# Layer 0 of two attention layers: the bias product of two rows in seven block products instead of eight

## The chip, the cores and the metric

The kernel runs on one core of a Trainium2 chip. The metric is the device time of one execution in microseconds (us), from outside the program; the profile's span runs from the first to the last instruction of one profiled execution. All arithmetic is float32.

## The reference

Two residual layers act on a tensor x of 128 rows of 256 tokens of 256 channels. The change is in the first, here cut to what matters (`_gn` is a group normalization over all rows and tokens):

```python
bias = jnp.einsum('nijz,zh->nhij', pair_repr, bias_proj)[:, None]
gate = jax.nn.sigmoid(msa_repr @ gate_proj).reshape(bs, s, r, head, c)   # 8 heads of 32
q, k, v = jnp.split(msa_repr @ qkv_proj, 3, axis=-1)
sim = jnp.einsum('nsqhc,nskhc->nshqk', q, k) * scale
sim = jax.nn.softmax(sim, axis=-1)
sim = sim + bias                       # added after the softmax, the same for all rows s
attend = jnp.einsum('nshqk,nskhc->nsqhc', sim, v) * gate
out = attend.reshape(bs, s, r, cm) @ out_proj
# x = x + layer0(_gn(x)); then x = x + layer1(_gn(x)), a banded attention of 4 heads
```

Since the bias is added after the softmax, `attend` is a softmax part, exp(sim) @ v divided by the sums, and a bias part, bias @ v. The bias is the same for every row, so for two rows together the bias part is, for each head, a 256 x 256 matrix (query by key) times the values of both rows: a product of 2 x 2 blocks by 2 x 2 blocks (key halves, query halves, the two rows).

## The kernel before

A first stage (to about 205 us) reads pair_repr and x, builds the bias in SBUF (`bias_sb`: partition = key within a half, then key half, head, query) and the statistics of x. Then a loop over the 128 rows s computes layer 0, and a second loop layer 1. In layer 0 the orders of TensorE (PE), ScalarE (ACT), VectorE (DVE) and of the DMA queue of SyncE (SP) are those of the program text (`tc.manual_schedule`); GpSimd (POOL) gets its order from the scheduler. A TensorE tile of 128 x 32 is a column strip: four products for four heads, or four quarters of an output, run side by side in the four strips, and float32 takes two instructions for each product.

Every row has the same frame, and rows go in pairs i = s // 2, of an even and an odd row. In row s, in TensorE's order:

- `scores(s, 0)`: scores of four heads (`sim`), which ScalarE turns into `ex` by exp; VectorE joins the two key halves (`both`, L862).
- `sum_heads(s - 1)` (`zs`, L885), the sums over keys; `divide(s - 1)` takes the reciprocal on VectorE (`rz`, L904), sends it to DRAM and back, spread over partitions (`near`, L910).
- `attend(s - 1)` (`av`, L872), the softmax part; then `scores(s, 1)`, the other four heads.
- a `stretch`, which computes two of the four projections for the next pair in seven products each (`two_of_them`): q and k in even rows, v and g (the gate) in odd rows. Each product adds into one of two halves of a PSUM bank, and ScalarE copies a half out (`take`: "15" after products 1 and 5, "6" and "7" into `mid`, "34") before the next product adds into it. GpSimd then adds the copies together (L631, L634). In odd rows the output projection of an earlier pair (`po`, seven products too, taken by VectorE at L704 to L726) is woven in.
- `bias_products(s - 1)` (`bv`, L872), the bias part of one row in two halves, put between the last products of the stretch by `between`.

On VectorE, `gated(s - 2)` heads the row: the bias part is added (L964, reading `bv` in PSUM), and the gate is applied (L965, writing `at`). `normal(s + 4)` transposes and normalizes a coming row (L553, L821). `weighted(s - 1)` multiplies `av` by `near` (L953). ScalarE's `totals` (L930) reads the sums `zs` once with an accumulator read. GpSimd's `row_sums` (L582 to L584) forms four sums of blocks that the seven products need: `ts` for the projections, `att` for the output.

PSUM has five banks in a ring for scores and projections and one each for `av`, `zs` and `bv`.

Of the kernel before, what the change touches and what calls it, by code (L numbers as in the profile page):

```python
# [15 lines left out]
P = 128  # L16
# [23 lines left out]
def conv_preact_kernel(  # L40
# [594 lines left out]

    def two_of_them(pool, f, g, name, po, rest, between):

        for p in (f, g):
            p.open()
            p.product(1)  # L640
            p.product(5)
            p.take("15")
        rest()
        twos = proj_bank(f"p2{name}")
        two = pool.tile([P, 2, R], F32, tag="two", name=f"two{name}", bufs=1)
        f.product(2, twos[:, 0, :], first=True)
        next(po, None)
        for p in (f, g):
            p.product(3)
            p.product(6)  # L650
            p.take("6")
            next(po, None)
        f.product(7)
        f.take("7")
        g.product(2, twos[:, 1, :])
        next(po, None)
        g.product(7)
        g.take("7")
        f.product(4)
        f.take("34")  # L660
        next(po, None)
        for work in between[:1]:
            work()
        g.product(4)
        g.take("34")
        nc.scalar.copy(two, twos)
        next(po, None)
        for work in between[1:]:
            work()
        next(po, None)  # L670
        for n, p in enumerate((f, g)):
            p.add_two(two[:, n, :])
            p.add_mid()
# [103 lines left out]
    with ExitStack() as both:  # L777
# [4 lines left out]
        quarters1["o"] = Quarters(st1, w_out_t, 0, "1o")  # L782
        big1 = both.enter_context(tc.tile_pool(name="big1", bufs=2))
        ygs, pools = {}, {}
        rz_far = dram.tile([2, 2, 4, R], F32, name="rz_far")
        rz0_far = dram.tile([2, A, 2, R], F32, name="rz0_far")

# [11 lines left out]
        with ExitStack() as lay0:  # L799
# [5 lines left out]

            xns, tss, res, ats, ats_t = {}, {}, {}, {}, {}

# [24 lines left out]
            def scores(s, half):  # L832
# [3 lines left out]
                for kt in range(2):  # L836
                    for c in range(2):
                        for j in range(4):
# [6 lines left out]
                            )  # L845
                ex = att.tile([P, 4, 2, R], F32, tag="ex", name=f"ex{s}_{half}", bufs=4)
                both = att.tile([P, 4, R], F32, tag="both", name=f"both{s}_{half}")
# [15 lines left out]

            def products(to, s, weights, halves=range(2)):

                i, r = divmod(s, 2)
                v = res["v", i]
                for half in halves:
                    for kt in range(2):
                        for j in range(4):  # L870
                            c0 = kt * P + j * D0
                            nc.tensor.matmul(  # L872
                                to[D0 * j : D0 * (j + 1), half, :],
                                lhsT=v[:, 2 * r + half, c0 : c0 + D0], rhs=weights(4 * half + j, kt),
                                start=(kt == 0), stop=(kt == 1),
                            )
# [13 lines left out]

            def bias_products(s):

                if s < 0:
                    return ()
                bv0 = hd[s] = ps_av.tile([P, 2, R], F32, tag="bv", name=f"bv{s}")
                return tuple(
                    lambda half=half: products(bv0, s, lambda h, kt: bias_sb[:, kt, h, :], (half,)) for half in range(2)
                )

            def divide(s, zs):  # L900
# [3 lines left out]
                nc.vector.reciprocal(rz, zs[:, 0, :])  # L904
                near = att.tile([P, 2, R], F32, tag="near", name=f"near{s}")
                if s < S - 1:
# [48 lines left out]
            def gated(s):  # L955
# [4 lines left out]
                if r == 0:  # L960
                    ats[i] = row.tile([P, 4, R], F32, tag="at", name=f"at{i}")
                st[s]["at"] = at = ats[i][:, 2 * r : 2 * r + 2, :]
# [11 lines left out]
            def output(i, amid):  # L974

                g, k = divmod(2 * i, XG)
                if k == 0:
                    outs[g] = big1.tile([P, XG, 2, R], F32, tag="o", name=f"o{g}")
                return Output(
# [5 lines left out]
            def finish(s):  # L985

                g, k = divmod(s, XG)
                if k == 0:
                    outs[g] = big1.tile([P, XG, 2, R], F32, tag="o", name=f"o{g}")
                nc.vector.tensor_tensor(outs[g][:, k], st[s]["po"], st[s]["xt"], ALU.add)  # L990
                settle(s, k, k, S // 2 - 1 + k % 2)
# [12 lines left out]

            def stretch(names, i, po=iter(()), rest=lambda: None, between=()):

# [3 lines left out]
                for w, p in zip(names, (f, g)):  # L1010
                    res[w, i] = p.to
                two_of_them(row, f, g, f"{names}{i}", po, rest, between)

# [6 lines left out]
            with tc.manual_schedule(  # L1020
# [4 lines left out]
                sum_rows(0)  # L1025
                stretch("qk", 0)
                for s in range(2, 4):
                    normal(s)
                stretch("vg", 0)
                sum_rows(1)  # L1030
                most1 = Most(st1, stats1, 3, 1)
                for s in range(S):
# [6 lines left out]
                    if s % 2 == 1:  # L1039
                        e = res["g", s // 2]  # L1040
                        nc.scalar.activation(e, e, AF.Tanh, scale=0.5)
                    attend(s - 1)
                    join_tiles(s, 0, 2)
                    if s % 2 == 0:
                        settle_pair((s - 4) // 2)
# [4 lines left out]
                    if s == 4:  # L1050
                        for weights in quarters1.values():
                            weights.sum()
                    late = (lambda: join_tiles(s, 1, 0), lambda: join_tiles(s, 1, 2), lambda: weighted(s - 1), lambda: least(s - 1))
                    bias = bias_products(s - 1)

# [6 lines left out]
                    if s % 2 == 1 and s > 1:  # L1062
                        out_sums((s - 3) // 2)
                        po, late = output((s - 3) // 2, late), ()
                    if s < S - 2:
                        stretch(("qk", "vg")[s % 2], s // 2 + 1, po, rest, bias)
                    else:
                        rest()
                        for work in bias:
                            work()  # L1070
                        for _ in po:
                            pass
                    for work in late:
                        work()
                    if s % 2 == 1 and s < S - 1:
                        sum_rows((s + 3) // 2)
                load1(0)
                load1(1)
# [10 lines left out]
                attend(S - 1)  # L1089
                for work in bias_products(S - 1):  # L1090
                    work()
                spread_last(S - 1)
# [16 lines left out]
        with ExitStack() as lay:  # L1109
            ps_av = psum(lay, "1", 4, 0)  # L1110
            pools["yg"] = lay.enter_context(tc.tile_pool(name="yg1", bufs=1))
            row = lay.enter_context(tc.tile_pool(name="row1", bufs=4))
# [368 lines left out]
    with tc.If(sure < P):  # L1481
        with ExitStack() as lay:
# [4 lines left out]
            for t in range(2):  # L1487
# [4 lines left out]
                out=bv_row.rearrange("p a b -> p (a b)"), in_=b_in[2 * C : 3 * C].partition_broadcast(P)  # L1492
            )
            stats2 = one.tile([P, 2, S // 2, 6], F32, name="stats2")

# [166 lines left out]
```

## Time and profile before

| | |
|---|---|
| median of 3 runs | 3122.66 us (3121.35 to 3122.96) |
| profiled execution | 3117.48 us, its span 3115.8 us |
| TensorE clock granted | 0.993 of full speed |
| pairs of layer 0 | from 205.9 us; layer 1's first work at 2044.1 us |
| group of instructions of the bias product (L872 bv) | 4096 instructions, 267.7 us busy |
| group of the attend product (L872 av) | 4096 instructions, 244.5 us busy |

Times are from the start of the span. "Busy" of a group is the time in which at least one of its instructions ran. The matrix instructions of the four strips overlap, so the mean of one (379 ns for 256 columns, 273 ns for 128 columns) is not what it adds to the queue; for that, the distance from one step's start to the next is read. PEld is TensorE's loading of weights, which runs beside the products. A "pair" below is the stretch of time from the first scores of an even row to those of the next even row.

### The profile page before, as it was taken

To read this page: it belongs to the slowest core of one execution; us is meant where nothing else is said; L and a number is where in the kernel's file an instruction comes from. 1 tells how busy PE (TensorE), PEld (TensorE's weight loads), DVE (VectorE), ACT (ScalarE), POOL (GpSimd) and SP (SyncE) were. 2 spreads that over 40 slices of the span, in tenths; PEclk is the share of its full clock that TensorE was granted. 3 is DMA by queue.
4 is the path that set the end of the run, shared out by engine and by line. 5 is a ranking of instruction groups with operands and counts; after the bars stand their busy time and mean duration, and the time that the engine had idled before them with its cause. 6 is when DMAs were issued, how large, how long until landed. Compare 5 with 4: busy or idle time off the path is not lost.

```text
span 3115.8 us, 135366 instructions
## 1 busy us (share of the span) xinstructions
PE 3038.3 (98%) x59661; PEld 1995.8 (64%) x59661; DVE 2176.2 (70%) x4327; ACT 1828.6 (59%) x4065; POOL 1718.3 (55%) x1660
## 2 busy tenths in 40 slices
PE   7889999999999999999999999999999999999997
PEld 4556566556656665665666566567777777777775
DVE  4667777777777777777777777746666666666665
ACT  4666666666666666666666666545555555555553
POOL 3035555545454555545454555457776777777774
PEclk9999999999999999999999999999999999999999
DMA  9942222222222222222222212124444444444443
GB/s 373 424 130 58 61 48 63 62 62 49 64 61 50 61 64 61 47 64 61 56 56 64 61 49 63 50 63 95 100 103 98 104 95 100 104 99 103 96 99 71
DMA packets 383716, 279.87 MB, mean 90 GB/s; under 512 B 285216, under 2 KB 352272, under 8 KB 376976
## 3 DMA queue, kind: packets, MB, share of 16 engines
q1 hardware_dynamic: 382224, 268.76, 33.1%
q8 instruction: 470, 7.70, 1.1%
q0 software_dynamic: 752, 2.36, 0.2%
q14 instruction: 126, 1.03, 0.1%
q10 hardware_dynamic: 144, 0.00, 0.0%
HBM read 202.38 MB, written 68.66 MB: 87 GB/s over the span
## 4 chain that ended last, share of the span: by engine, by line
PE 92%; DMA 4%; DVE 2%; ACT 1%; issue 0%; POOL 0%; SPq 0%; DVEq 0%; ACTq 0%; POOLq 0%
PE sim L840 9%; PE av L872 7%; PE bv L872 7%; PE p1v L1184 7%; PE p1q L590 7%; PE po L590 6%; PE p1k L590 6%; PE p1o L590 6%; PE pq L590 6%; PE pv L590 6%; PE pk L590 5%; PE pg L590 5%; PE zs L885 4%; DMA pr<-in_L_conv_pair_repr_dram 4%; PE 1sim L1205 3%; PE 1av L1246 3%
## 5 line engine op out<-in xcount | busy, mean ns | idle before, releaser
L853 ACT ACTIVATE ex<-sim 128x512 f32<-128x512 f32 x1024 | 550.2, 608 | 318.4 <-PE sim L840 318.4
L862 DVE TENSOR_TENSOR both<-ex 128x512 f32<-128x512 f32 x512 | 402.0, 813 | 15.1 <-ACT ex L853 15.0
L634 POOL TENSOR_TENSOR q<-q,midq 128x512 f32<-128x512 f32 x64 | 82.0, 1281 | 443.3 <-ACT q L628 443.3
L634 POOL TENSOR_TENSOR v<-v,midv 128x512 f32<-128x512 f32 x64 | 81.6, 1276 | 415.6 <-ACT v L628 415.6
L840 PE MATMUL sim<-q,k 32*64 32x256 f32 x8192 | 288.9, 387 | 1.4 <-ACT ex L853 1.3
L872 PE MATMUL bv<-bias_sb,v 128*32 128x256 f32 x4096 | 267.7, 379 | 0.0
L904 DVE RECIPROCAL rz<-zs 128x256 f32<-128x256 f32 x128 | 224.3, 1753 | 32.9 <-PE zs L885 32.9
L872 PE MATMUL av<-ex,v 128*32 128x256 f32 x4096 | 244.5, 379 | 0.1
L1215 POOL TENSOR_TENSOR 1p<-1ex,seen 128x768 f32<-128x768 f32 x127 | 231.5, 1823 | 12.8 <-ACT 1ex L1213 12.8
L1184 PE MATMUL p1v<-w_in_t,1xn 128*64 128x128 f32 x4096 | 236.2, 273 | 0.1
L1184 PEld LDWEIGHTS p1v<-w_in_t,1xn 128*64 128x64 f32 x4096 | 231.4, 137 | 6.1 <-issue 0.5
L840 PEld LDWEIGHTS sim<-q,k 32*64 32x64 f32 x8192 | 151.9, 131 | 127.4 <-issue 104.1
L697 ACT ACTIVATE 1q<-p1q,bqk 128x256 f32<-128x256 f32 x192 | 90.9, 473 | 240.8 <-PE p1q L590 129.7
L582 POOL TENSOR_TENSOR 1ts<-1xn 128x512 f32<-128x512 f32 x64 | 81.4, 1271 | 231.6 <-ACT 1xn L1145 231.6
L872 PEld LDWEIGHTS av<-ex,v 128*32 128x32 f32 x4096 | 133.4, 110 | 87.9 <-issue 0.6
L872 PEld LDWEIGHTS bv<-bias_sb,v 128*32 128x32 f32 x4096 | 133.6, 110 | 87.5 <-DVE both L862 0.4
L964 DVE TENSOR_TENSOR t<-bv,t 128x512 f32<-128x512 f32 x128 | 87.9, 687 | 131.0 <-PE bv L872 130.9
L1315 DVE TENSOR_TENSOR 1at<-1av,1near 128x512 f32<-128x512 f32 x128 | 82.6, 686 | 136.3 <-DMA 1near<-rz_far 115.3
L1222 POOL TENSOR_TENSOR 1zp<-1p 128x512 f32<-128x512 f32 x127 | 162.4, 1279 | 10.0
L726 DVE TENSOR_TENSOR o<-po,xt 128x256 f32<-128x256 f32 x189 | 80.3, 425 | 98.9 <-PE po L590 98.9
L1191 ACT COPY 1v<-p1v 128x512 f32<-128x512 f32 x128 | 75.0, 586 | 125.1 <-PE p1v L1184 125.1
L346 DVE BATCH_NORM_STATS2 stats<-xs 128x6 f32<-128x128 f32 x512 | 100.3, 278 | 65.3 <-DMA xs<-in_x_dram 65.3
(320 smaller groups left out, 7826.1 us busy)
## 6 DMA issues: line engine op xcount, KB each, us to landing
pr<-in_L_conv_pair_repr_dram SPq DMA_DIRECT2D x32, 1024.0 KB
xs<-in_x_dram SPq DMA_DIRECT2D x16, 2048.0 KB
x<-o SPq DMA_DIRECT2D x64, 512.0 KB
yg<-x SPq DMA_DIRECT2D x64, 512.0 KB
out_dram<-1o SPq DMA_DIRECT2D x256, 128.0 KB
near<-rz_far SPq DMA_DIRECT2D x508, 64.0 KB
xg<-in_x_dram SPq DMA_DIRECT2D x252, 128.0 KB
1near<-rz_far SPq DMA_DIRECT2D x124, 256.0 KB
```

Of the source, the lines that this page charges most:

```text
L346: nc.vector.bn_stats(out=stats[:, g, n, :], in_=xs[:, 0:k, g * CG : (g + 1) * CG])
L590: nc.tensor.matmul(out[cols], lhsT=lhsT[:, cols], rhs=rhs, **flags)
L634: nc.gpsimd.tensor_tensor(self.to[:, 2:4], self.to[:, 2:4], self.mid, ALU.add)
L840: nc.tensor.matmul(sims[j][KB * c : KB * (c + 1), kt, :], lhsT=k[p0 : p0 + D0, 2 * r + half, k0 : k0 + KB], rhs=q[p0 : p0 + D0, 2 * r + ha ...
L853: nc.scalar.activation(ex[:, j], sims[j], AF.Exp, scale=1.0 / math.sqrt(D0))
L862: nc.vector.tensor_tensor(both[:, j : j + 2], ex[:, j : j + 2, 0, :], ex[:, j : j + 2, 1, :], ALU.add)
L872: nc.tensor.matmul(to[D0 * j : D0 * (j + 1), half, :], lhsT=v[:, 2 * r + half, c0 : c0 + D0], rhs=weights(4 * half + j, kt), start=(kt == ...
L885: nc.tensor.matmul(zs[strip(j), 0, :], lhsT=place0[:, half, :], rhs=both[:, j, :], start=(half == 0), stop=(half == 1),)
L904: nc.vector.reciprocal(rz, zs[:, 0, :])
L1184: nc.tensor.matmul(ps[KB * half : KB * (half + 1), b, :], lhsT=xns[i][:, 2 * r + kt, KB * b : KB * (b + 1)], rhs=w_in_t[:, kt, 2 * C + P * ...
L1215: engine.tensor_tensor(p.rearrange("p j (r c) -> p (j r) c", c=WROW)[:, :, 0 : 2 * WSTEP] .rearrange("p r (t c) -> p r t c", c=WSTEP)[:, : ...
L1222: engine.tensor_tensor(zp, p[:, :, 0:R], p[:, :, R : 2 * R], ALU.add)
```

## The change

The bias part is now computed for two rows at once, by `biased(i)`, in seven block products instead of eight (a product of 2 x 2 blocks in the manner of Strassen and Winograd). Its parts:

- The sums of bias blocks are kept: `sum_bias` forms three new blocks and overwrites one block of `bias_sb` with a difference, once, by VectorE in row 0. The block that is overwritten is stored to DRAM first (`bias_far`), and read back in the branch for unusual data at the program's end.
- The sums of the values are formed for each pair by GpSimd (`sum_values`, four operations of 128 x 256), after the odd row's stretch.
- Each of the seven products is eight matrix products of 128x32 weights by 128 columns. Two products at a time use the two halves of the PSUM bank `bv`; after each product, ScalarE copies (2, 6, 5 and 4) or VectorE adds (1, 7 and 3), into SBUF tiles `bv0`, `bv1` and `midb`. `gated` reads the bias part from there instead of from PSUM.
- The products are spread over the pair: 2, 1 and 6 in the even row's stretch; 5 in the odd row between `sum_heads` and `attend`; 7, 3 and 4 in the odd row's stretch. They belong to the pair itself, not to the row before.
- The order of a stretch is now written as a string. In it fA and gA are products 1 and 5 with their copy, x is ScalarE's last exp and `totals`, f and g with a number are products (2 of g with the copy of both), b a bias product, p an output product, d one of the late VectorE works (two joins, `weighted`, `least`). In even rows product 2 of f moves from behind gA to behind f7; in odd rows product 2 of g moves from behind f7 to behind g4.
- Buffers: `ex` 3 instead of 4, `near` 1 instead of 2, `at` 1 instead of 2, the layer 0 output tile `o` 1 instead of 2 (its pool `big1` is opened for layer 1 only). New tiles: `vt`, `bv0`, `bv1`, `midb`, `bias_sums`.
- In the last two rows, which have no stretch, the bias products stand among the output products; nothing of the bias part is left behind the loop.

```diff
+    PLAIN = "fA gA x f2 p f3 f6 p g3 g6 p f7 b p g7 f4 p b g4 p g2 b p"
+    EARLY = "fA gA x d b f3 f6 g3 g6 d f7 f2 g7 f4 b d g4 g2 d b"
...
-                ex = att.tile([P, 4, 2, R], F32, tag="ex", name=f"ex{s}_{half}", bufs=4)
+                ex = att.tile([P, 4, 2, R], F32, tag="ex", name=f"ex{s}_{half}", bufs=3)
...
+            bias_of = {
+                1: bias_blocks[0, 0], 2: bias_blocks[1, 0], 4: bias_blocks[1, 1],
+                3: bias_sums[:, 2], 5: bias_sums[:, 0], 6: bias_sums[:, 1], 7: bias_blocks[0, 1],
+            }
+            def sum_bias():
+                w00, w10, w01, w11 = (bias_blocks[kb, m] for m in range(2) for kb in range(2))
+                s1, s2, s4 = (bias_sums[:, n] for n in range(3))
+                nc.vector.tensor_tensor(s1, w01, w11, ALU.add)
+                nc.vector.tensor_tensor(s2, s1, w00, ALU.subtract)
+                nc.vector.tensor_tensor(s4, w10, s2, ALU.subtract)
+                nc.vector.tensor_tensor(w01, w00, w01, ALU.subtract)
+            def sum_values(i):
+                v = res["v", i]
+                vts[i] = row.tile([P, 4, 2, P], F32, tag="vt", name=f"vt{i}", bufs=1)
+                by_key = v.rearrange("p (r h) (k c) -> p k r h c", r=2, k=2)
+                t = vts[i]
+                for h in range(2):
+                    nc.gpsimd.tensor_tensor(
+                        t[:, 0::2, h], by_key[:, :, 1, h], v[:, h::2, 0:P], ALU.subtract
+                    )
+                nc.gpsimd.tensor_tensor(t[:, 1], by_key[:, 1, 1], t[:, 0], ALU.subtract)
+                nc.gpsimd.tensor_tensor(t[:, 3], by_key[:, 1, 0], t[:, 1], ALU.subtract)
+            def biased(i):
...
+                for n in (2, 1, 6, 5, 7, 3, 4):
+                    acc = 1 if n in (2, 3, 5) else 0
+                    for half in range(2):
+                        for j in range(4):
+                            nc.tensor.matmul(
+                                ps[strip(j), acc, half, :],
+                                lhsT=stationary[n][:, half, strip(j)], rhs=bias_of[n][:, 4 * half + j, :],
+                                start=(n <= 2 and half == 0), stop=(n in (2, 3, 4)), skip_group_check=True,
+                            )
...
+                    if n == 2:
+                        nc.scalar.copy(to[0][:, 0], ps[:, 1])
+                    elif n == 1:
+                        nc.vector.tensor_tensor(to[0][:, 0], ps[:, 0], to[0][:, 0], ALU.add)
+                    elif n == 6:
+                        nc.scalar.copy(mid, ps[:, 0])
+                    elif n == 5:
+                        nc.scalar.copy(to[1][:, 1], ps[:, 1])
+                    elif n == 7:
+                        nc.vector.tensor_tensor(to[1][:, 1], ps[:, 0], to[1][:, 1], ALU.add)
+                    elif n == 3:
+                        nc.vector.tensor_tensor(to[1][:, 0], ps[:, 1], mid, ALU.add)
+                    else:
+                        nc.scalar.copy(to[0][:, 1], ps[:, 0])
+                    yield
...
-                near = att.tile([P, 2, R], F32, tag="near", name=f"near{s}")
+                near = att.tile([P, 2, R], F32, tag="near", name=f"near{s}", bufs=1)
...
+                    if s % 2 == 0:
+                        bias = biased(s // 2)
+                    else:
+                        next(bias)
                     attend(s - 1)
                     join_tiles(s, 0, 2)
+                    if s == 0:
+                        sum_bias()
...
-                    bias = bias_products(s - 1)
...
-                    if s % 2 == 1 and s < S - 1:
+                    if s % 2 == 1 and s < S - 2:
                         sum_rows((s + 3) // 2)
+                        sum_values(s // 2 + 1)
...
-                for work in bias_products(S - 1):
-                    work()
```

## The prediction

> **What bounds the kernel now.** I read the busy times first, then the stretches, then the chain that ended last, then the timeline of one pair of rows. The page gives TensorE 98% of the span and nobody else over 70%. The stretch answer (columns: length; busy time of TensorE, weight loads, VectorE, ScalarE, GpSimd; clock, DMA share, GB/s) shows the steady part of layer 0.
>
> ```profile
> PE 3038.3 (98%) x59661; PEld 1995.8 (64%) x59661; DVE 2176.2 (70%) x4327; ACT 1828.6 (59%) x4065; POOL 1718.3 (55%) x1660
> ...
> 231.18:2004.85 1773.67, 1773.61 (x38692) 1067.29 (x38689) 1324.88 (x2163) 1120.53 (x2419) 917.04 (x869) 1.00 0.25 58
> ```
>
> 62 pairs in 1773.67 us are 28.61 us a pair, and TensorE lacks 0.06 us in all. So a pair costs what TensorE's queue costs, and a change counts only as it shortens that queue or makes it wait. The chain over one pair is TensorE alone, with each step's own length:
>
> ```profile
> 1009.27 0.86 PE pk L590 x16
> 1010.13 0.43 PE p2qk L590 x8
> 1010.56 0.94 PE pq L590 x16
> ...
> 1014.09 0.86 PE bv L872 x16
> ```
>
> A product of a 128x256 operand is 0.43 us; a half of a row's bias product (16 instructions) is 0.86. The 0.94 hides a wait. The timeline (start, length, engine, work; in brackets the idle time before and what ended it) shows it, and the places where the others are tight:
>
> ```profile
> 1004.64 1.20 DVE L965 SCALAR_TENSOR_TENSOR at<-g,t 128x512 f32<-128x512 f32 x1
> ...
> 1007.42 1.53 DVE L862 TENSOR_TENSOR both<-ex 128x512 f32<-128x512 f32 x2
> ...
> 1010.43 0.16 PEld L590 LDWEIGHTS pq<-xn,sums_q 128*32 128x32 f32 x8 [0.35 <-ACT q L622]
> ...
> 1011.20 0.45 ACT L930 ACTIVATE z<-zs 128x256 f32<-128x256 f32 x1
> 1011.37 1.28 DVE L862 TENSOR_TENSOR both<-ex 128x512 f32<-128x512 f32 x2
> 1011.47 0.26 ACT L930 ACTIVATION_READ_ACCUMULATOR z<-zs 128x1 f32 x1
> ...
> 1011.63 0.37 ACT L624 COPY midq<-pq 128x256 f32<-128x256 f32 x1
> ...
> 1012.05 0.27 PEld L590 LDWEIGHTS pq<-ts,sums_q 128*32 128x32 f32 x8 [0.16 <-ACT midq L624]
> ...
> 1014.82 1.28 POOL L634 TENSOR_TENSOR q<-q,midq 128x512 f32<-128x512 f32 x1 [7.02 <-ACT q L628]
> ...
> 1023.64 0.62 PE L590 MATMUL pv<-sums_v,xn 128*32 128x128 f32 x16
> 1023.89 0.42 DVE L726 TENSOR_TENSOR o<-po,xt 128x256 f32<-128x256 f32 x1 [0.43 <-PE po L590]
> 1024.07 0.62 PE L590 MATMUL pv<-sums_v,ts 128*32 128x128 f32 x16
> ```
>
> See: ScalarE runs without a gap up to midq, and a weight load of the q product 7 starts 0.05 after midq ends. GpSimd is idle for 7 us before q+midq. VectorE is 0.43 early at an odd row's first output add. A v product, 16 instructions 128 columns wide, starts 0.43 after the one before.
>
> **What the skill says.** The Trainium skill, "TensorEngine Tiling (Array Packing)", Key Properties: changing the tiling mode drains TensorE. The new products keep the 128*32 form, so no change of form is added; the trace has the price at the scores (bias half at 1015.21, scores at 1016.18: 0.97 for 0.86). The skill, "SBUF — State Buffer", SBUF: two separate sides: VectorE and GpSimd share a port pair; an operation with two SBUF inputs, or in a 2-port mode, and a GpSimd operation exclude each other ("the other fully blocks"). The trace agrees: two joins of `both` take 1.53 where they meet the end of GpSimd's work and 1.28 where they don't, and the gating (L965) 1.20 beside GpSimd; the bias add (L964, from PSUM) takes 0.68 beside busy GpSimd.
>
> **The change part by part.** Times are those of the pair above (even row from 1003.37, odd from 1016.18).
>
> *Bias product on TensorE.* Before, four halves a pair, 4 x 0.86 = 3.44. After, 7 products of 16 instructions 128 columns wide. Their price is the v product's 0.43, the same weights and width; different moving data in the four strips is what the old bias product has too, at full rate. 7 x 0.43 = 3.01: -0.43 a pair, over 64 pairs **-27.5 us**. If the rate failed by 0.05 a product, 0.35 a pair would be gone.
>
> *ScalarE: four copies of 128x256 a pair*, 1.5 us where it is idle 10.5 of 28.6 (stretch of one pair: busy 18.07). Product 5's sits after the tanh, 6's and 4's at the end of a stretch, before scores it waits 0.7 to 1.7 us for: nothing, and if that idle time went, up to 0.27 each. Product 2's is different: it goes between the read of the totals and midq. One 256-wide operation pushes the next by 0.27 (1011.20 to 1011.47). So midq ends at 1012.27, not 1012.00, while product 7 of q, in the same place since bias product 2 replaces product 2 of q before it, has its turn at 1012.18. From the 0.94 above: the q copy ended (9.77+0.61) just when that step was due, and the queue lost 0.08. So q's product 7 starts at 1012.35: **+0.17 a pair**, x63 = +10.7. Bounds 0.05 to 0.3.
>
> *VectorE: three adds of 128x256 from PSUM a pair* (0.42, the output adds' row), with 7.2 us idle of 28.6. Two come in odd rows between output adds: 0, as each meets 0.3 to 1.3 us of waiting for `po`; if that cover went, 0.42 would be late for the next output product. The third (product 1) gates product 6, which adds into the same half bank. With product 7's wait, product 1 ends at 1014.8, the add at 1015.25, product 6's turn is 1015.43: 0.1 spare, if the add starts at once. Ahead of it in VectorE's queue stand the joins of the second scores; behind it the scaling by the sums, already waiting for its DMA (it began at 1013.64) and not needed until 1016.3.
>
> *GpSimd: four sums of 128x256*, 0.73 each (ts, L583, without contention): 2.9 us, in the 7 us idle before 1014.82; bounds 2.9 to 4.8 (1.19 each, L631 beside VectorE). Their readers: product 6 at 1015.4, sums ready by about 1012.6. One goes ahead of adding product 2 to v; that still ends near 1008.7, before bias product 2 at 1009.95. The cost is the port. Also the bias add now reads SBUF twice, so it takes part. For the even row I count a gating that ends 0.9 later (two operations, each held about half a GpSimd operation), the first two joins +0.55, the normalization +0.3: the second joins end at 1014.4 instead of 1012.65. That is 0.4 before product 1's add: 0. For the odd row the gating ends 0.6 later, the reciprocal, which waits for the sums (1018.37), about as before; then out_sums start later and meet both joins in full, +0.65, so the first output add, 0.43 early, is about 0.2 late: VectorE still finishes 0.1 before the next output product needs it. 0, bounds -0 to +0.3 a pair.
>
> *Buffers.* ex 4 to 3: the third buffer is free when the attend product is through, and the scores stand behind that on TensorE. near, at: their readers precede the next write on the same engines by whole rows. o: its store (issued 1011.90) shares in traffic that is over by 1018 (stretch 1018 to 1020: 6 GB/s), the next write is at 1024. All 0; without that cover the output add would wait for the store.
>
> *SP:* one more store of 512 KB, once, ahead of x loads that are four rows early: 0. The reload stands in a branch that isn't taken.
>
> *Start.* VectorE sums the bias, 4 operations of 128x1024, 1.2 each (twice 0.68 less one start), and sharing the port with seven GpSimd operations: 8 us or so in row 0, ahead of the normalization, the joins and product 1's add. Product 6 then stands about 4 us, and the ts sums delay two products by 0.9: **+5** (2 to 8).
>
> *End.* Row 126 has three products in a row without cover: product 6 waits for an add behind bn_aggr (1011.05+1.82 after 2000), +2.6, of which the following wait for the joins returns half; the last row's bias leaves the path to `near` (-0.65); layer 1's first tiles now wait for the last store: +1.5 against the plain count (-1 to 4).
>
> **Sum:** -27.5 + 10.7 + 5 + 1.5 = **-10.3 us**. The profiled execution took 3117.48 (span 3115.8), 5.2 below the median 3122.66; the same difference from the median gives 3112.4.
>
> **Rivals.** *Full gain:* ScalarE's copy starts are 0.05 to 0.1 closer and product 7 doesn't wait: -27.5+6.5 = -21, 3102. For: 0.1 of slack stood before midq; against: the queue has no gap there. *GpSimd's sums run into q+midq (slower):* if the even row's chain is 1.3 us later than I count, the last join (start 1013.7) asks for the port after q+midq took it at 1015.0. It ends at 1016.85, product 1's add at 1017.2, and product 6 waits 1.85 us for it in each pair: 62 x 1.85 = +115, less 10: 3225. It decides from a GpSimd sum of about 1.1 instead of 0.73. For: L631's 1.19; against: 1.3 us of room. *Small waits add up (no change or a little slower):* 0.1 to 0.3 a pair at product 6 and the first output add, where spare is 0.1: +6 to +19, so 3118 to 3131.
>
> **How the numbers follow.** Forecast 0.47, full gain 0.13, small waits 0.27, collision 0.13. 0.2% is 6.2 us, about what a measurement of this kernel can tell from no change. Faster takes the forecast, the full gain and none of the rest: 0.60; small waits split 0.12 same, 0.15 slower; with the collision slower is 0.28. The range 3098 to 3131 leaves out the collision and a few per cent below.
>
> **What would show it.** The steady pair at 28.35 (28.17 without product 7's wait); 0.17 more before q's product 7, put down to midq; no TensorE wait on the add of product 1; joins at L859 longer, about 0.9 mean. Wrong, if TensorE idles on VectorE at bias product 6 or at `po`, or bias products start over 0.45 apart.

## The result, and the profile after

The changed kernel took 3123.47 us (median; 3121.14 to 3128.69), the kernel before 3121.93 on the same chip (3116.97 to 3124.77): ratio 1.0009, 95% interval 1.0000 to 1.0017. The forecast of 10 us less did not come. The profiled execution took 3121.14, its span is 3119.4 us.

The stretches of the changed kernel's profile (columns as in the prediction): the first two pairs, the 61 pairs that follow, the last two rows with what leads into layer 1, and layer 1.

```profile
207.10:241.13 34.03, 26.98 (x572) 16.38 (x569) 20.26 (x23) 20.39 (x43) 19.62 (x16) 0.90 0.04 10
241.13:270.93 29.80, 29.27 (x677) 18.10 (x673) 26.29 (x39) 19.69 (x45) 21.33 (x20) 1.00 0.16 39
270.93:2008.79 1737.86, 1737.60 (x40997) 1103.38 (x40993) 1535.30 (x2314) 1174.58 (x2624) 1183.03 (x1099) 1.00 0.25 59
2008.79:2050.09 41.30, 33.38 (x542) 19.60 (x539) 33.07 (x60) 14.03 (x31) 8.54 (x10) 0.96 0.25 79
```

| stretch | before | after | difference | forecast |
|---|---|---|---|---|
| ahead of the first scores | 205.92 | 207.10 | +1.2 | 0 |
| first two pairs | 53.86 | 63.83 | +10.0 | +6.0 |
| 61 pairs | 1745.07 | 1737.86 | -7.2 | -15.9 |
| last two rows and what leads into layer 1 | 39.24 | 41.30 | +2.1 | -0.5 |
| layer 1 | 1071.7 | 1069.3 | -2.4 | 0 |
| span | 3115.8 | 3119.4 | +3.6 | -10.3 |

The forecast column splits the prediction's sum by stretch, which the prediction itself did not do: 5 for the sums of the bias, and 1.3 for bias products that now stand in the first pair and no longer at the end; -0.26 for each steady pair; what is left of the sum falls to the last rows. Layer 1's work did not change; over all profiles below it takes 1069.1 to 1072.5. Ahead of the first scores stand only a store, the first pair's sums of the values and a new order of the same products. The first scores begin at 205.0 and 205.9 in the two profiles with the old row loop, at 206.1 to 207.5 in the six that have the new loop alone, and at 208.1 to 209.0 in the three that also sum the bias there (e4, f1, f2). So the change, and the early sums too, may cost a microsecond or two ahead of the loop; no run parts that from the spread.

The 61 pairs gain, but half of what was forecast: the steady pair is **28.47** us (28.60 before, 28.35 forecast). TensorE's busy time fills the stretch in both kernels, so that column can't show where the rest went. The chain over one even row of the changed kernel can (start, length of the step in the queue, step):

```profile
1018.28 0.44 PE pbv L933 x16
1018.72 0.99 PE pq L590 x16
1019.71 0.86 PE pk L590 x16
1020.58 0.60 PE pq L590 x8
...
1023.77 0.49 PE pbv L933 x16
```

A bias product is 0.44 where nothing is in its way, a q product 0.43. Three steps are longer than that count: the two q products 3 and 6 (0.99; 0.94 before), q's product 7 (0.60; 0.43 before) and bias product 6 (0.49). The timeline of that row shows what each is near:

```profile
1016.45 2.07 DVE L859 TENSOR_TENSOR both<-ex 128x512 f32<-128x512 f32 x2
...
1018.64 0.16 PEld L590 LDWEIGHTS pq<-xn,sums_q 128*32 128x32 f32 x8 [0.19 <-ACT q L622]
...
1019.77 0.43 ACT L943 COPY bv<-pbv 128x256 f32<-128x256 f32 x1
...
1020.12 0.37 ACT L624 COPY midq<-pq 128x256 f32<-128x256 f32 x1
...
1020.54 0.16 PEld L590 LDWEIGHTS pq<-ts,sums_q 128*32 128x32 f32 x8 [0.44 <-ACT midq L624]
...
1023.05 0.42 DVE L945 TENSOR_TENSOR bv<-pbv,bv 128x256 f32<-128x256 f32 x1 [0.63 <-PE pbv L933]
...
1023.59 0.41 PEld L933 LDWEIGHTS pbv<-bias_sums,vt 128*32 128x32 f32 x16 [0.30 <-issue]
```

Product 2's copy (L943) stands ahead of midq, and q's product 7 waits for midq, as forecast. But the q product 3 is late too, which was not, and product 6's first weight load begins 0.12 after product 1's add has ended, with "issue" as the reason: no other engine's work ended there.

The start, in the timeline of row 0:

```profile
212.23 1.75 DVE L901 TENSOR_TENSOR bias_sums<-bias_sb 128x1024 f32<-128x1024 f32 x1
...
217.25 1.75 DVE L904 TENSOR_TENSOR bias_sb<-bias_sb 128x1024 f32<-128x1024 f32 x1
...
221.26 3.41 DVE L859 TENSOR_TENSOR both<-ex 128x512 f32<-128x512 f32 x2
222.42 1.70 POOL L634 TENSOR_TENSOR k<-k,midk 128x512 f32<-128x512 f32 x1
...
224.60 0.41 DVE L945 TENSOR_TENSOR bv<-pbv,bv 128x256 f32<-128x256 f32 x1
225.16 1.08 PE L933 MATMUL pbv<-bias_sums,vt 128*32 128x128 f32 x16 [5.25 <-DVE bv L945]
226.17 2.01 PE L837 MATMUL sim<-q,k 32*64 32x256 f32 x32
```

The four sums take 6.8 us of VectorE. The two joins come behind them and meet GpSimd's adding of q and k: 3.41 for what takes 1.28 alone. TensorE waits 5.25 us, and the scores after that run at half pace (2.01 for 1.12): the trace has the clock at half from 223.7 to 230.5 us, which makes the 0.90 of this stretch. The Trainium skill, "TensorE: Matmul & The Clock Gate", The HAM clock gate (the "warmup" mystery), says that TensorE's clock falls to half after an idle window of about 3.4 us; this wait and the scores behind it agree.

### The profile page after: what moved, and what is told of

The parts are those of the page before. It is cut to its first block, busy times and chain, and to the rows that moved or that the text cites. A ratio compares the mean times of both kernels' runs of the same rounds, so it can differ in the third digit from the quotient of the medians.

```text
span 3119.4 us, 142735 instructions
## 1 busy us (share of the span) xinstructions
PE 3028.8 (97%) x62733; PEld 2048.6 (66%) x62733; DVE 2422.4 (78%) x4523; ACT 1904.3 (61%) x4321; POOL 2015.4 (65%) x1916
## 4 chain that ended last, share of the span: by engine, by line
PE 91%; DMA 5%; DVE 2%; POOL 1%; issue 1%; ACT 0%; SPq 0%; DVEq 0%; POOLq 0%; ACTq 0%
PE sim L837 8%; PE p1v L1260 7%; PE av L869 7%; PE p1q L590 7%; PE pbv L933 6%; PE po L590 6%; PE pq L590 6%; PE p1o L590 6%; PE p1k L590 6%; PE pv L590 6%; PE pk L590 5%; PE pg L590 5%; PE zs L882 4%; PE 1sim L1281 3%; DMA pr<-in_L_conv_pair_repr_dram 3%; PE 1av L1322 3%
## 5 line engine op out<-in xcount | busy, mean ns | idle before, releaser
L859 DVE TENSOR_TENSOR both<-ex 128x512 f32<-128x512 f32 x512 | 471.0, 948 | 13.4 <-ACT ex L850 13.2
L1023 DVE SCALAR_TENSOR_TENSOR at<-g,t 128x512 f32<-128x512 f32 x128 | 202.6, 1583 | 9.2 <-DVE t L1022 0.5
L882 PE MATMUL zs<-both,place 128*32 128x256 f32 x2048 | 138.8, 388 | 0.5 <-DVE both L859 0.5
L688 DVE SCALAR_TENSOR_TENSOR 1o<-p1o,bo_v,yg 128x256 f32<-128x256 f32 x183 | 88.5, 483 | 56.0 <-PE p1o L590 53.2
```

The lines of the kernel that those rows point to most:

```text
L859: nc.vector.tensor_tensor(both[:, j : j + 2], ex[:, j : j + 2, 0, :], ex[:, j : j + 2, 1, :], ALU.add)
L882: nc.tensor.matmul(zs[strip(j), 0, :], lhsT=place0[:, half, :], rhs=both[:, j, :], start=(half == 0), stop=(half == 1),)
L1023: nc.vector.scalar_tensor_tensor(at, res["g", i][:, 2 * r : 2 * r + 2, :], 1.0, t, op0=ALU.add, op1=ALU.mult)
```

## The experiments

Four theories of the lost time. **A**: product 2's copy ahead of midq, the forecast's own term. **A1**: the third `ex` buffer puts something ahead of the exponentials. **The port**: GpSimd's sums of the values lengthen VectorE's work until product 6 is late. **C**: the sums of the bias in row 0. In the table, the steady pair is the commonest length; times of single executions have no interval. e3, e6, e7 and e8 leave terms out of the bias part or use wrong ones, and show times alone.

| kernel | steady pair | first two pairs | last rows | time | before, same chip |
|---|---|---|---|---|---|
| e1: copy behind midq | 28.31 | 63.86 | 41.17 | 3111.81 | 3122.72 |
| e2: kernel before, three `ex` | 28.60 | 53.86 | 41.01 | 3119.05 | 3122.72 |
| e3: the first pair's sums of the values for all | 28.42 | 64.05 | 40.46 | 3117.34 | 3122.72 |
| e4: sums of the bias early | 28.47 | 56.65 | 41.94 | 3116.82 | 3122.72 |
| e6: four `ex`, no sums of the bias | 28.41 | 54.93 | 41.20 | 3110.14 | 3120.81 |
| f1: e1 and e4 | 28.31 | 54.96 | 41.30 | 3106.51 | 3120.81 |
| f2: f1 and the last rows | 28.31 | 56.48 | 39.00 | 3107.90 | 3120.81 |
| e7: e1, e3 and e6 | 28.20 | 54.88 | 40.69 | 3096.89 | 3122.00 |
| e8: e7, sums made but not read | 28.20 | 54.82 | 43.43 | 3099.87 | 3122.69 |

**e1: product 2's copy behind midq.** Product 2 of q goes back to its place before the change, and the bias product 2 takes the later one.

```diff
-    EARLY = "fA gA x d b f3 f6 g3 g6 d f7 f2 g7 f4 b d g4 g2 d b"
+    EARLY = "fA gA x f2 d f3 f6 g3 g6 d f7 b g7 f4 b d g4 g2 d b"
```

> In the even row, bias product 2 moves from ahead of product 3 of q to behind product 7 of q, and product 2 of q goes back to where it was before the change; so ScalarE copies bias product 2 behind the second mid copy of q and no longer ahead of the first. Theory A (ScalarE's queue ahead of the mid copy of q makes TensorE wait): q's product 7 follows the product before it at 0.43 instead of 0.58, so the steady pair falls from 28.475 to 28.28 to 28.33 us, about 10 us over the program. Theory B (the shared port of GpSimd and VectorE holds TensorE in the even row): the pair stays at 28.4 to 28.5.

The pair fell from 28.47 to 28.31: 0.16 for the order of one copy, which the prediction put at 0.17. q's product 7 moved from 9.01 to 8.87 after the row's first scores, but not to the 8.81 of the kernel before: midq still began at 8.31 instead of 8.25. So something ahead of midq on ScalarE costs another 0.06. The first two pairs did not change. The step of q's product 7 in a steady pair of e1, 0.60 in the chain above:

```profile
1045.28 0.43 PE pq L590 x8
```

**e2: the kernel before with three `ex` buffers.**

```diff
-                ex = att.tile([P, 4, 2, R], F32, tag="ex", name=f"ex{s}_{half}", bufs=4)
+                ex = att.tile([P, 4, 2, R], F32, tag="ex", name=f"ex{s}_{half}", bufs=3)
```

> The kernel before with three ex buffers instead of four, nothing else. Theory A1 (the third buffer makes the exp of the second scores wait on one more signal and start 0.06 us later, which passes to the q copy and to TensorE's product 3 of q): the steady pair grows from 28.60 to 28.65 to 28.70 us, 3 to 6 us over the program. Rival (the later exp comes from elsewhere): 28.60.

Not a hundredth in the pair. I took that for the end of A1; e6 shows why it was too early. What this run says is that the third buffer alone, in the old order of work, costs nothing in the pair. The last rows were 1.8 longer than in the kernel before. Most of that is the clock: it is at half from 2027.0 to 2030.4 us, in the kernel before it is full there, and the steps of the last row's sums and attend product took 3.89 for 2.59.

**e3: the first pair's sums of the values for all pairs.** 

```diff
             def sum_values(i):
                 v = res["v", i]
+                if i > 0:
+                    vts[i] = vts[0]
+                    return
...
-                v, t = res["v", i], vts.pop(i)
+                v, t = res["v", i], vts[i]
```

> The changed kernel with GpSimd's four sums of the values formed for the first pair alone; all later pairs use those of the first pair, so 2.9 us of GpSimd work a pair are left out and nothing else. Theory A (only ScalarE's order costs TensorE time in a steady pair): 28.47, unchanged, while VectorE's joins get shorter (mean 948 ns towards 810 to 870). Theory B (the shared port costs it): the pair falls to 28.2 to 28.3 us.

The joins (L859) fell from 948 to 880 ns, and the pair by 0.05, all of it at product 6 and the scores behind it. That looks like the port, but e3 takes away two things: the traffic, and product 6's wait for GpSimd. e8 parts them. The trace of e3 speaks for the wait already:

```profile
1022.05 0.42 DVE L948 TENSOR_TENSOR bv<-pbv,bv 128x256 f32<-128x256 f32 x1 [1.38 <-PE pbv L936]
...
1022.52 0.41 PEld L936 LDWEIGHTS pbv<-bias_sums,vt 128*32 128x32 f32 x16 [0.23 <-DVE bv L948]
```

Product 1's add runs from 11.52 to 11.94 after the row's first scores in both kernels, so the traffic did not delay it. Only the weight load behind it came closer: 0.05 after the add's end, for 0.12 in the changed kernel.

**e4: the sums of the bias ahead of the row loop**, in waits of the start-up.

```diff
             def sum_bias():
...
                 nc.vector.tensor_tensor(s4, w10, s2, ALU.subtract)
+                yield
                 nc.vector.tensor_tensor(w01, w00, w01, ALU.subtract)
+                yield
...
                 for s in range(2):
                     normal(s)
+                nc.sync.dma_start(out=bias_far, in_=bias_blocks[0, 1])
                 sum_rows(0)
+                bias_work = sum_bias()
+                next(bias_work)
                 stretch("qk", 0, EARLY)
                 for s in range(2, 4):
                     normal(s)
+                next(bias_work)
...
-                    if s == 0:
-                        sum_bias()
```

> The changed kernel with the sums of the bias moved from row 0 to ahead of the loop, where VectorE waits for the first rows (three sums behind the first two normalizations, the difference behind the next two). Theory C (the first two pairs are long because these four operations and the port stand ahead of the joins and of product 1's addition): the first two pairs together fall from 63.83 to 54.5 to 56 us, the steady pair stays 28.475, the first scores begin at most 1 us later; about 8 us over the program. Rival (the first pairs are long for the reason that three bias products and the values' sums come there at all): they fall by less than 3 us.

The first two pairs lost 7.2 of their extra 10.0, the steady pair none: C holds, and apart from A, though 56.65 is just above the 54.5 to 56 expected. Some of what is left is the clock: 0.94 in the first pair of this profile, 1.00 in f1's, where the two pairs took 54.96.

**e6: four `ex` buffers, without the sums of the bias**, whose room the fourth buffer needs.

```diff
-                ex = att.tile([P, 4, 2, R], F32, tag="ex", name=f"ex{s}_{half}", bufs=3)
+                ex = att.tile([P, 4, 2, R], F32, tag="ex", name=f"ex{s}_{half}", bufs=4)
...
-            bias_sums = row.tile([P, 3, H0, P], F32, tag="bias", name="bias_sums", bufs=1)
...
-                3: bias_sums[:, 2], 5: bias_sums[:, 0], 6: bias_sums[:, 1], 7: bias_blocks[0, 1],
+                3: bias_blocks[0, 0], 5: bias_blocks[1, 0], 6: bias_blocks[1, 1], 7: bias_blocks[0, 1],
...
-                    if s == 0:
-                        sum_bias()
```

> The changed kernel with four ex buffers again, and, to make room for the fourth, without the sums of the bias: products 3, 5 and 6 take single blocks of the bias where sums belong, and sum_bias is gone, so the output lacks those terms; the instructions of the row loop are otherwise the same. Theory A1 (with three ex buffers the first exp of the second scores has to name a second semaphore, which puts one more instruction of 0.06 us ahead of it on ScalarE): the exp starts 0.06 earlier in the even row, q's product 3 at 7.06 instead of 7.12 after the row's scores, steady pair 28.41 if q's product 7 follows, 28.47 if that one's wait for midq takes it up again. Rival: ex buffers have no part in it, product 3 stays at 7.12 and the pair at 28.47. First pair about 7 shorter in both, since sum_bias is gone, so near 3114.

28.41: A1 holds after all, for 0.06. A line's view counts the semaphore instructions that stand ahead of its work in the engine's queue (count, then shortest, median and longest in ns). First the exponentials of the changed kernel:

```profile
L850 ACTq EVENT_SEMAPHORE  x129: 17/17/38, 207.3 to 2026.5; - x129
```

The same of e6, and then of e2:

```profile
L850 ACTq EVENT_SEMAPHORE  x2: 17/28/38, 207.4 to 207.5; - x2
```

```profile
L853 ACTq EVENT_SEMAPHORE  x129: 17/17/38, 205.2 to 2012.3; - x129
```

With three buffers, an exponential in nearly every row has to wait on two semaphores, and one of the two waits is put ahead of it in an instruction of its own. Which exponential, and which wait, is not the same in the two kernels. The trace names the semaphores.

In the changed kernel it is the first exponential of the second scores. The wait put ahead is the one for TensorE's scores, the later of the two; the other, for ScalarE's own earlier work, stays with the exponential. ScalarE is idle until the scores come, and then the extra instruction runs first. The changed kernel, and then e6:

```profile
1016.54 1.57 ACT L850 ACTIVATE ex<-sim 128x512 f32<-128x512 f32 x3 [1.77 <-PE sim L837]
```

```profile
1005.83 1.57 ACT L850 ACTIVATE ex<-sim 128x512 f32<-128x512 f32 x3 [1.71 <-PE sim L837]
```

So the exponential begins 0.06 later (5.01 after the row's first scores instead of 4.95). From there to midq ScalarE has no gap: q's copy ends at 7.07 instead of 7.01, and the q product 3 that needs its place starts at 7.12 instead of 7.06. In e6 all these are back. In odd rows the exponential is 0.06 late too, but there no step of TensorE grows. (e6 changes two things, but the sums of the bias are made in row 0 alone.)

In e2 it is the second exponential of the first scores, and the wait put ahead is for VectorE. It is over at 1.31 after the row's first scores, while ScalarE still computes the first exponential (from 1.18 on), and the second begins at 1.67 with and without it. The four run in one piece:

```profile
1004.01 2.07 ACT L853 ACTIVATE ex<-sim 128x512 f32<-128x512 f32 x4 [1.69 <-PE sim L840]
```

**f1: e1 and e4 together.** The edits are those of the two.

> The changed kernel with both single cures together: the bias products' copies in the order of e1 (product 2's ScalarE copy behind midq instead of ahead of it) and the sums of the bias made in the waits ahead of the row loop as in e4. If the causes are separate (my theory), their gains add: steady pair 28.31 as in e1, first two pairs about 56.5 (63.83 - 7.2 - 0.15), so about 7.2 + 62 x 0.16 = 17 us less than the changed kernel, near 3105 (3102 to 3109), ratio to the kernel before 0.994 to 0.996. Rival: they overlap (the early bias sums gain nothing more than the start-up DMA gives back, first scores +1 to +2 later): near 3110 to 3112, as e1 alone.

28.31 and 54.96, the two gains beside each other: 3106.51 us, ratio to the kernel before 0.9958 (0.9943 to 0.9972). This version beats both kernels, the one before by 0.4%.

**f2: f1, and the last two rows put right.**

```diff
-                    if S - 3 <= s < S - 1:
-                        most1.join(s - S + 3)
+                    if s == S - 3:
+                        most1.join(0)
...
+                        if s % 2 == 0:
+                            next(bias)
...
-                        for _ in range(2 if s % 2 == 0 else 3):
+                        for _ in range(1 if s % 2 == 0 else 3):
...
+                most1.join(1)
```

> f1 and the last rows put right too: in row 126 the next bias product is started before the rest of the row's output work, and the last join of the values' sums is moved behind the attention of the last row, so that the add of product 1 and of product 6 no longer stand behind the row's statistics on VectorE. Theory (the change's loss at the end is product 1's 2.28 wait and product 6's 1.78 wait in row 126): rows 126, 127 and the tail fall from 41.3 to 38 to 40, total 1.5 to 3 less than f1, near 3102 (3099 to 3106), ratio 0.9935 to 0.995. Rival: the tail is set by the last row's values and softmax sums, and the time only moves from row 126 into row 127: equal to f1 within 0.5.

In row 126 of f1, product 1 and product 6 wait:

```profile
2000.66 0.65 PE L935 MATMUL pbv<-bias_sb,v 128*32 128x128 f32 x16 [2.28 <-ACT bv L945]
...
2003.09 0.77 PE L935 MATMUL pbv<-bias_sums,vt 128*32 128x128 f32 x16 [1.79 <-DVE bv L947]
```

In f2:

```profile
2002.07 0.64 PE L935 MATMUL pbv<-bias_sb,v 128*32 128x128 f32 x16 [1.44 <-ACT bv L945]
...
2003.42 0.64 PE L935 MATMUL pbv<-bias_sums,vt 128*32 128x128 f32 x16 [0.71 <-DVE bv L947]
```

The last rows fell by 2.3 to 39.00, as expected of the stretch. The two waits make up 1.9 of it; the clock, at half from 2003.5 to 2006.9 us in f1, stayed full in f2, and the next row's scores took 1.12 instead of 2.01. The time did not follow: 3107.90, ratio 0.9957 (0.9945 to 0.9969), which can't be told from f1. In f2's profile the first two pairs were 1.5 longer, the first of them at a clock of 0.94, and layer 1 was 2.3 longer (1072.5 to 1070.2), in code that is the same; a gain of 2.3 is below what these runs part.

**e7: e1, e3 and e6 together**, to close the account of the steady pair. The edits are those above.

> Three single edits in one kernel, to close the account of the steady pair: the order of e1 (copy of product 2 behind midq), one pair's sum of the values for all (e3), and four ex buffers with no sums of the bias (e6). The output lacks what e3 and e6 leave out. Alone they took 0.16, 0.05 and 0.06 from the pair's 28.47. Theory (three separate costs, which with about 0.02 in the odd row are all that stands between the changed kernel and the bare count of 28.60 - 0.43 = 28.17): 28.20, within 0.02, with q's product 3 at 7.06 and its product 7 at 8.81 after the row's scores, where they lie in the kernel before. Rivals: they overlap, since each only uncovers the next late operand: 28.25 to 28.31; or another wait of the change stays behind them, with the pair above 28.25 and a place of its own in the trace.

28.20: the three are separate costs (0.16 + 0.05 + 0.06 from 28.47), and what remains over the bare count of 28.17 is 0.03. That is no wait: the seven products are a little dearer than counted, 0.437 each. q's product 3 and product 7 are at 7.06 and 8.81, where the kernel before has them.

**e8: e7 with GpSimd's sums back, written to a tile that nothing reads.**

```diff
-                if i > 0:
-                    vts[i] = vts[0]
-                    return
-                vts[i] = row.tile([P, 4, 2, P], F32, tag="vt", name=f"vt{i}", bufs=1)
...
-                t = vts[i]
+                vts[i] = vts.get(0)
+                t = row.tile([P, 4, 2, P], F32, tag=f"vt{min(i, 1)}", name=f"vt{i}", bufs=1)
+                if i == 0:
+                    vts[0] = t
```

> The kernel of e7 with GpSimd's four sums of the values back in every pair, written to a tile of their own that nothing reads; products 4, 6 and 7 still read the first pair's sums, so the output lacks what e7 lacks. It parts two readings of e3's 0.05: in the changed kernel product 6 waits for two semaphores (VectorE's add, GpSimd's sums), and one more instruction of 0.05 stands ahead of its first weight load at 11.98 to 12.06 after the row's scores; e3 took away that wait and the port traffic together. If the second wait is the cost: 28.20 as in e7, though the joins go back up from 878 ns to about 945, and no semaphore instruction ahead of product 6. If the traffic on the port is the cost: 28.25, with product 6 late behind product 1's add.

Still 28.20, with the joins back from 878 to 930 ns. So it is not the port. (In e8 GpSimd's sums meet VectorE less: 0.74 for each of the first two, 0.96 in the changed kernel. That product 1's add came no later in the changed kernel than in e3 says the same without e8.) The chain of e8 over the even row, the steps that were long:

```profile
1002.08 0.94 PE pq L590 x16
1003.01 0.86 PE pk L590 x16
1003.88 0.43 PE pq L590 x8
...
1006.91 0.44 PE pbv L934 x16
```

The view of the bias products' line in the changed kernel, and in e8 (PEldq is TensorE's queue for weight loads):

```profile
L933 PEldq EVENT_SEMAPHORE  x65: 51/51/51, 225.1 to 2018.9; - x65
```

```profile
L934 PEldq EVENT_SEMAPHORE  x2: 51/51/51, 217.8 to 230.6; - x2
```

Product 6 needs VectorE's add, which frees its half bank, and GpSimd's sums. The sums are ready 2.7 us before the add ends, but they are a second semaphore. By the trace's semaphores it is again the later wait, for the add, that is put into an instruction of its own. It starts at 11.98 after the row's scores, 0.04 after the add's end, takes 51 ns, and the first weight load follows at 12.06. In e3, e7 and e8 the load itself waits for the add and starts 0.05 after its end.

## Why the prediction was wrong

The span came out 13.9 us above the forecast (+3.6 for -10.3): 8.7 of it in the 61 pairs, about 4 in the first two, 2.5 at the end, and -1.2 in the two stretches for which nothing was forecast.

**The count was right, its price a little low.** Seven products for eight take 0.40 from a pair: e7 and e8, without the three small costs, stand at 28.20 against 28.60. The prediction counted 0.43, with 0.43 for a product and 0.86 for a half. Over many pairs a product of either kind, the v product's and the bias product's, is 0.437 and a half 0.864; seven of the one for four of the other is 0.40.

**ScalarE's copy ahead of midq was right**: +0.17 forecast, 0.16 measured (e1).

**The steady pair failed in two terms costed at nothing.** *Buffers* put `ex` 4 to 3 at 0, since the third buffer is free in time. It is; but an exponential then waits on two semaphores, and the instruction that this adds takes over the wait for the scores, behind which ScalarE has no gap up to midq: 0.06 a pair (e6). *VectorE* put product 6 "0.1 spare, if the add starts at once", and the add was in time; but product 6 waits on two engines: 0.05 (e3, parted by e8). Both have the same form: a second semaphore that is long satisfied still costs an instruction, and in both places that instruction carries the wait that ends last. The Trainium skill, "Perfetto Trace Analysis", Identifying Dependency Chains, says that instructions which wait on several engines may get such instructions put ahead of them; it gives no price, the runs give 0.06 and 0.05. The prediction looked for late operands and did not count waits. With the 0.03 of the products, less 0.01 that midq cost less than forecast, these are 0.13 of the 0.26 forecast, or 7.9 us of the 8.7 that the 61 pairs fell short; the rest is mostly a few longer pairs.

**The start was too small**: +5 (2 to 8), measured 8.9 from e1 to f1, which differ in the place of the sums. The time of VectorE in row 0 was about right (6.8 for the sums, about 8 forecast), and so was the wait at product 6 (5.25, about 4 forecast). Left out was that the joins behind them meet GpSimd's adding of q and k, which is the slower rival's collision, once instead of in each pair, and that TensorE's clock falls to half behind that wait.

**The end was too small**: the stretch was forecast at -0.5 and came at +2.1. The wait of product 6 for an add behind the aggregation was named (+2.6; 1.78 measured). That product 1 would wait 2.28 for product 2's copy, which ScalarE makes only behind the row's last exponential, was not. f2 recovers 2.3 of the stretch. Left out too was the clock: it is at half from 2019.1 to 2022.5 us, behind these waits, and in the kernel before it is full. GpSimd's sums have a share here: in e3 product 6 waits 0.73 instead of 1.78, as the two joins ahead of its add take 1.22 and not 2.17, the clock stays full in row 126, and the row lasts 9.71 us for 11.11. The third `ex` buffer has none: e6, with four, has 41.20. How much is the wait for product 1 and how much the clock was not parted.

**The port behaved as forecast in the steady pair.** Joins at 948 ns (about 0.9 forecast), the sums of the values at 962 ns in their first form (0.73, bounds to 1.19), GpSimd 4.6 us more a pair (1183.03 less 900.29, over 61; bounds 2.9 to 4.8), and none of it on the path of the steady pair. The rival of small waits gave the right time, 3118 to 3131, and the right place for one of them, product 6; it gave the wrong cause, and the first output add, its other place, cost nothing. That its time came true was luck: product 6 cost 0.05 a pair, below its 0.1 to 0.3, and most of the loss stood elsewhere.

## What to carry to other kernels

When an edit removes a buffer or lets an instruction read a further engine's result, ask of that instruction how many semaphores it now waits on, not only whether they are ready. A second one is an instruction more in that engine's queue. Here it was free where it could run while the engine was still busy with earlier work (e2), and cost 0.05 to 0.06 us, times the trips of the loop, where it carried the wait that ends last and the work behind it had no slack. When an engine's busy time fills its stretch, read the lengths of the steps in the chain against the same steps elsewhere: 0.60, 0.49 and 0.99 among 0.43, 0.44 and 0.94 held the whole answer. Work that is done once belongs into a wait that exists, here the start-up, and not ahead of the first row's own work.

## What was not expected of the hardware

- An extra wait of 17 ns stands ahead of an exponential 127 times in the row loops of both e2 and the changed kernel (the views count two more at the start). In e2 it is passed during the exponential before and costs nothing; in the changed kernel it holds the wait for the scores and moves the exponential by 0.06. Why one wait or the other is put ahead is open.
- VectorE's busy time rose by 230.5 us in the 61 pairs (1304.76 to 1535.30), 3.8 a pair, of which three adds are 1.3, and the pair did not feel it. The joins at 930 instead of 878 ns (e8, e7) left it at 28.20.
- Two joins that met two GpSimd operations took 3.41 us, for 1.28 alone.
- TensorE's clock fell to half in row 126 of f1 behind waits of 2.28 and 1.79 us with one product of 0.65 between them, neither as long as the 5.25 of row 0. Behind 1.44 and 0.71 (f2), or 2.28 and 0.73 (e3), it stayed full.
